# Graph layer on one core: the token term moves from TensorE matmuls to ScalarE pre-fills and GpSimd row additions

## The chip, the cores and the metric

The kernel runs on one core of a Trainium2 chip. The metric is the device time of one execution in microseconds (us); the time before is the median of three runs, 2477.9 us (2477.26 to 2478.84). Engines are named as in the profile: PE is TensorE's matmuls and PEld its weight loads, DVE is VectorE, ACT is ScalarE, POOL is GpSimd, SP is SyncE, which issues the DMAs.

## What is computed

There are 64 samples of 256 tokens with 768 features, and a 256x256 adjacency matrix for each. It is 0 or 1 here, and the same matrix serves as `heads` and as `rels`. Cut to what matters:

```python
h = relu(layernorm(x))
ctx = (adj  @ (h @ Wadj.T + badj)) / deg_c  + (radj @ (h @ Wrev.T + brev)) / rdeg_c
ctx = ctx + h @ Wself.T + bself
rel = agg @ Wr.T + br * deg + ragg @ Wrr.T + brr * rdeg     # agg = sum_j adj_ij * E[rels_ij]
out = x + ctx + rel
```

`deg` and `rdeg` are row sums of the adjacency and of its transpose, `deg_c` and `rdeg_c` the same with 0 replaced by 1. Since every edge has relation 1, `agg @ Wr.T` is the degree times one fixed row of 768 numbers (a row of `E` through `Wr`), and likewise for the reverse term. So beside the large products there is a **token term**: a row `bself`, a row `badj` where `deg > 0`, a row `brev` where `rdeg > 0`, and two rows multiplied by `deg` and by `rdeg`.

## The kernel before, in words

**Tiling and stages.** A sample has two blocks of 128 tokens, c = 0 and 1. For each there are three output blocks of 128x768, `c{c}{m}`: m = 0 is h Wadj, m = 1 the result with h Wself (it starts from x), m = 2 is h Wrev. The product of the 256x768 h with the three weight matrices is split by a bilinear scheme into 15 smaller products, each of three passes over words of split precision (4 matmuls a pass, 12 a product). The first sweep (`SWEEPS[0]`, 8 products) goes over all regular samples 1 to 62, its five partial blocks are kept in DRAM, then the prepared weight words are exchanged and the second sweep (`SWEEPS[1]`, 7 products) goes over all samples again and ends with the aggregation. Samples 0 and 63 are done whole, by plain matmuls (`whole`), sample 63 in the exchange between the sweeps.

**A product** (`product`): `split` makes the left words (ACT left0, DVE left1 and left2; in the second sweep the two DVE steps have two SBUF inputs, L613 and L617), PE runs the first passes into a PSUM bank, ACT rescales the bank in place (L666), PE adds the second passes (L628), and DVE or ACT reads the bank into the blocks (L676, L685, L687). Some left inputs are sums of two pieces that POOL makes first (`combine`, L590).

**The aggregation** (`high_low`, `aggregate`): a block is split in two words, the high one by ACT (L928) and the low one by POOL (L932). For each of two directions k and two token blocks ic, 8 matmuls (L944) of the adjacency with the words fill a bank, and DVE adds bank times 1/degree to the result block `c{ic}1` (L955). That is 32 matmuls a sample beside 84 of the seven products.

**The token term before.** `front2` puts 16 small columns (flags, ones, degrees) into `cols` (L910, L911), PE transposes them (L915), ACT copies the result as the token tile (L919). `add_rows` (L638) multiplies four 32-row tiles of it by `rows`, a tile made once in `rows_prepare`, into the banks of products 7 and 15 (v and u), after both of their passes; the second read of each of the two banks (`read(1)`) is held until then. Samples 0 and 63 get the term in banks of their own (L981).

**Order.** A planner (`Plan.schedule`) records all steps with a rank, a duration and the buffers they need, and emits one fixed order for each engine. The table `OFFSETS` shifts the rank of each kind of step. Steps marked `lock` (all of POOL's, and DVE's with two SBUF inputs) are never placed at the same time. `SLOTS` gives the number of buffers of a class: B are 128x768 blocks in SBUF, Q are PSUM banks in pairs. Semaphores keep the data dependencies at run time; each engine goes through its own order.

## Time and profile before

| what | value |
|---|---|
| median of three runs | 2477.9 us |
| the profiled execution: its own time | 2478.37 us |
| span of the profiled execution | 2476.5 us |
| outside the span | 1.87 us |
| PE busy, share | 2449.1 us, 99% |
| PEld busy, share | 2365.0 us, 95% |
| DVE, ACT, POOL busy, share | 85%, 72%, 52% |
| granted TensorE clock | 0.999 |

Busy times are unions of the instructions' intervals. PE's matmuls are pipelined, so a single one is shown longer than the distance to the next; what counts on PE is the distance between starts.

### The profile page before, as it was taken

The numbers are of one execution on the slowest core, as the hardware profiler recorded it, in microseconds if no ns is written. First come the engines' busy times: TensorE is split into PE (matmuls) and PEld (weight loads), VectorE is DVE, ScalarE is ACT, GpSimd is POOL, SyncE is SP. The second block draws the span as 40 slices with busy tenths as digits, with TensorE's granted clock in tenths as the row PEclk, the third lists the DMA queues.
The fourth block names the chain that finished last, engine by engine and source line by source line (L and its number), as shares of the span: only waits on it lengthen the run. The fifth ranks groups of instructions, "written<-read, shape, count | busy, mean of one in ns | idle before, by whom it ended". The sixth has DMA issues, their size and how long they took to land.

```text
span 2476.5 us, 43288 instructions
## 1 busy us (share of the span) xinstructions
PE 2449.1 (99%) x13858; PEld 2365.0 (95%) x13858; DVE 2096.0 (85%) x4003; ACT 1777.2 (72%) x3772; POOL 1283.1 (52%) x1138
## 2 busy tenths in 40 slices
PE   6999999999999999999999999999999999999998
PEld 4899999999999999996999999999999999999998
DVE  7887888788788878878988889888888888888987
ACT  4788888888888888886666666666666666666665
POOL 1555555555555555543555555555555555555554
PEclk9999999999999999999999999999999999999999
DMA  5677777777777777876666666666666666666664
GB/s 214 241 284 281 268 277 284 271 274 282 277 268 280 285 270 275 293 254 215 223 214 216 216 217 212 216 217 215 213 213 213 216 215 216 217 216 214 215 219 135
DMA packets 224776, 590.66 MB, mean 239 GB/s; under 512 B 25080, under 2 KB 25080, under 8 KB 224544
## 3 DMA queue, kind: packets, MB, share of 16 engines
q1 hardware_dynamic: 224544, 587.86, 69.5%
q8 instruction: 110, 1.80, 0.3%
q14 instruction: 122, 1.00, 0.1%
HBM read 364.28 MB, written 223.48 MB: 237 GB/s over the span
## 4 chain that ended last, share of the span: by engine, by line
PE 97%; DVE 1%; DMA 1%; ACT 1%; issue 0%; POOL 0%; SPq 0%; ACTq 0%; POOLq 0%
PE x L628 21%; PE y L628 21%; PE agg L944 14%; PE z L628 10%; PE w L628 10%; PE t L628 5%; PE v L628 5%; PE u L628 5%; PE whole L782 2%; PE v L638 1%; DMA raw<-in_Wself_dram 0%; PE right L502 0%; PE pt L915 0%; DMA row<-d 0%; DVE right L555 0%
## 5 line engine op out<-in xcount | busy, mean ns | idle before, releaser
L932 POOL TENSOR_TENSOR hl<-c,hl 128x768 fp32r<-128x768 f32 x256 | 474.7, 1855 | 646.3 <-ACT hl L928 470.6
L628 PE MATMUL x<-word,left 128*128 128x384 f32 x2976 | 589.3, 339 | 0.2 <-DVE c L687 0.2
L628 PE MATMUL y<-word,left 128*128 128x384 f32 x2976 | 569.3, 335 | 0.0
L628 PEld LDWEIGHTS x<-word,left 128*128 128x128 f32 x2976 | 515.2, 188 | 14.2 <-issue 11.0
L628 PEld LDWEIGHTS y<-word,left 128*128 128x128 f32 x2976 | 517.8, 188 | 5.2 <-ACT y L666 1.0
L944 PE MATMUL agg<-hl,a 128*128 128x384 f32 x2048 | 395.3, 334 | 0.0
L944 PEld LDWEIGHTS agg<-hl,a 128*128 128x128 f32 x2048 | 358.4, 188 | 0.6 <-issue 0.2
L745 POOL TENSOR_TENSOR h<-h,row 128x768 f32<-128x768 f32 x128 | 234.6, 1855 | 177.5 <-DMA row<-d 132.2
L628 PE MATMUL z<-word,left 128*128 128x384 f32 x1488 | 299.3, 335 | 0.7 <-DVE x L793 0.4
L628 PE MATMUL w<-word,left 128*128 128x384 f32 x1488 | 298.2, 334 | 0.2 <-ACT w L666 0.2
L666 ACT ACTIVATE x<-x 128x768 f32<-128x768 f32 x248 | 191.8, 794 | 137.1 <-PE x L628 136.4
L628 PEld LDWEIGHTS z<-word,left 128*128 128x128 f32 x1488 | 258.7, 188 | 4.5 <-DVE x L793 0.7
L628 PEld LDWEIGHTS w<-word,left 128*128 128x128 f32 x1488 | 261.3, 188 | 0.8 <-ACT w L666 0.5
L955 DVE SCALAR_TENSOR_TENSOR c<-agg,rd,c 128x768 f32<-128x768 f32 x252 | 255.2, 1013 | 7.1 <-PE agg L944 3.9
L928 ACT ACTIVATE hl<-c 128x768 fp32r<-128x768 f32 x256 | 215.2, 841 | 30.9 <-DVE c L685 25.0
L666 ACT ACTIVATE y<-y 128x768 f32<-128x768 f32 x248 | 197.1, 795 | 41.5 <-PE y L628 41.4
L722 POOL TENSOR_TENSOR cols<-cols,half 128x2 f32<-128x2 f32 x64 | 83.0, 1296 | 252.7 <-DVE cols L721 252.7
L617 DVE SCALAR_TENSOR_TENSOR left<-left,top 128x256 fp32r<-128x256 f32 x496 | 199.5, 413 | 6.4
L685 DVE TENSOR_TENSOR c<-c,v 128x768 f32<-128x768 f32 x124 | 117.5, 947 | 102.0 <-PE v L628 101.1
L617 DVE SCALAR_TENSOR_TENSOR left<-left 128x256 fp32r<-128x256 f32 x434 | 203.3, 490 | 0.1
L607 ACT ACTIVATE top<-left 128x256 f32<-128x256 f32 x496 | 181.0, 383 | 6.2 <-DVE left L617 2.0
L676 ACT ACTIVATE c<-y 128x768 f32<-128x768 f32 x124 | 101.1, 815 | 70.0 <-PE y L628 69.9
(136 smaller groups left out, 4308.3 us busy)
## 6 DMA issues: line engine op xcount, KB each, us to landing
c<-kept SPq DMA_DIRECT2D x316, 384.0 KB
kept<-c SPq DMA_DIRECT2D x252, 384.0 KB
x<-in_x_dram SPq DMA_DIRECT2D x128, 384.0 KB
h<-in_x_t_dram SPq DMA_DIRECT2D x128, 384.0 KB
out_dram<-c SPq DMA_DIRECT2D x126, 384.0 KB
kept_h<-h SPq DMA_DIRECT2D x124, 384.0 KB
h<-kept_h SPq DMA_DIRECT2D x124, 384.0 KB
adj<-in_adj_dram SPq DMA_DIRECT2D x64, 512.0 KB
```

The lines of the kernel that those rows point to most:

```text
L607: lambda: nc.scalar.activation(view(top), t(w)[:, 0].bitcast(F32), AF.Copy),
L617: lambda: nc.vector.scalar_tensor_tensor(t(w)[:, 2], t(w)[:, 1].bitcast(F32), -STEP, first(), op0=ALU.mult, op1=ALU.add), s == 1,
L628: nc.tensor.matmul(t(q)[:, half, : H // 2], t(w)[:, lw, f, :], t(r[rw])[:, f, ts(half, H // 2)], start=start and i == 0 and f == 0, stop=s ...
L666: lambda: nc.scalar.activation(view(), view(), AF.Copy, scale=scale),
L676: lambda o=o, sign=sign: nc.scalar.activation(t(o).rearrange("p (k n) -> p k n", k=2), view(), AF.Copy, scale=sign * (1.0 if value_last el ...
L685: emit = lambda to=to, op=op: nc.vector.tensor_tensor(to(), to(), view(), op=op)
L722: pool(0.7, r - 21.5, f"pow {b}", [col], [col], lambda: nc.gpsimd.tensor_tensor(var(), var(), v["half"], op=ALU.pow))
L745: lambda h=h, one=one: nc.gpsimd.tensor_tensor(t(h), t(h), one(0), op=ALU.subtract),
L928: lambda: nc.scalar.activation(t(pair)[:, 0], t(o), AF.Copy, scale=LOWER),
L932: lambda: nc.gpsimd.tensor_tensor(t(pair)[:, 1], t(o), t(pair)[:, 0].bitcast(F32), op=ALU.subtract),
L944: nc.tensor.matmul(t(q)[:, half, : H // 2], t(s["a"])[:, c, k, ts(ic, P)], t(pairs[c])[:, part, ts(half, H // 2)], start=(c == 0 and part ...
L955: lambda q=q, to=to, ic=ic: nc.vector.scalar_tensor_tensor(to(), t(q)[:, :, : H // 2], t(rd)[:, ic, k : k + 1], to(), op0=ALU.mult, op1=AL ...
```

## The change

PE's token rows, the transposes and the token tiles are gone. In their place: (1) in each of the four aggregation banks of a sample ACT first writes a prepared row (`forward` or `reverse`) times the squared degree, and the 8 matmuls accumulate on that; the later multiplication by 1/degree makes it row times degree. (2) ACT writes the row `brev` into the banks of products 7 and 15 before their first matmul. (3) POOL adds `badj` to the blocks c00 and c10 of regular samples in the first sweep, and `bself` minus `brev` to c01 and c11 in the second; for samples 0 and 63 it adds all bias rows. (4) DVE computes the squared degrees (`sqd`) in place of the two column steps. (5) Five rows of 128x768 are loaded by broadcast DMAs in place of one small 5-row load issued eight times, and hold five B buffers from then on; B has 19 slots in place of 18. (6) The second reads of products 7 and 15 are no longer held back. (7) `OFFSETS` is a new table (741 of the 749 kinds that stay have another value), and the planner may widen its look-ahead where it would find no order. The diff, cut:

```diff
-SLOTS = {"W": 24, "B": 18, "T": 5, "A": 3, "S": 6, "Q": 4, "U": 2}
+SLOTS = {"W": 24, "B": 19, "T": 5, "A": 3, "S": 6, "Q": 4, "U": 2}
...
+            if not events and pace < 1000.0:
+                pace *= 2.0
+                continue
+            pace = PACE
...
-    def add_rows(b, rank, token, qs, start):
...
+    def add_row(name, o, rank, what):
+        row = v["row"][name]
+        pool(
+            on_pool(H), rank, what, [row, o], [o],
+            lambda: nc.gpsimd.tensor_tensor(t(o), t(o), t(row), op=ALU.add),
+        )
+
+    def load_row(name, at, rank):
+        row = v["row"][name] = plan.buf("B", [P, H], F32, f"row_{name}")
+        dma(384, rank, "bias", [], [row], lambda: nc.sync.dma_start(t(row), v["bias"][at].partition_broadcast(P)))
+        return row
...
+        fresh = place == 0
+        if n in (7, 15):
+            row = v["row"]["brev"]
+            act(
+                in_place(H), rank - 1.0, f"init {n} {b}", [row], [q],
+                lambda: nc.scalar.activation(view(), t(row).rearrange("p (k n) -> p k n", k=2), AF.Copy),
+            )
+            fresh = False
...
+                if m == 0:
+                    add_row("badj", o, rank + 3.0, f"bias{c}{m} {b}")
                 return
...
+        brev, bself = load_row("brev", 1, rank - 8.0), load_row("bself", 2, rank - 8.0)
+        per = [load_row(name, 3 + k, rank - 8.0) for k, name in enumerate(("forward", "reverse"))]
...
-        dve(0.2, r - 2.0, f"tok {b}", degs, [(col, 0)], lambda: nc.vector.tensor_scalar(to(0), of(), 0.0, None, op0=ALU.is_gt))
-        dve(0.2, r - 2.0, f"tok {b}", degs, [(col, 1)], lambda: nc.vector.tensor_copy(to(3), of()))
+        dve(0.2, r - 2.0, f"sqd {b}", degs, [sqd], lambda: nc.vector.tensor_tensor(t(sqd), t(deg)[:, b], t(deg)[:, b], op=ALU.mult))
...
-        pt = plan.buf("Q", [P, 2, 512], F32, f"pt2_{b}")
-        pe(0.3, r - 1.0, f"turn2 {b}", [col], [pt], lambda: nc.tensor.transpose(t(pt)[:, 0, :P], t(col), v["ident"]))
-        s["token"] = v["tokens"][b % 2]
-        act(
-            0.3, r - 0.5, f"token {b}", [pt], [s["token"]],
-            lambda: nc.scalar.activation(t(s["token"]), t(pt)[:, 0, :P], AF.Copy),
-        )
...
-                                start=(c == 0 and part == 0), stop=(c == 1 and part == 1),
+                                start=False, stop=(c == 1 and part == 1), skip_group_check=True,
...
+            row, sqd = v["row"][("forward", "reverse")[k]], v["sqd"][b % 2]
+            act(
+                in_place(H), rank - 1.5 + 1.4 * ic, f"init{k}{ic} {b}", [row, sqd], [q],
+                lambda q=q, ic=ic, row=row: nc.scalar.activation(
+                    t(q)[:, :, : H // 2], t(row).rearrange("p (k n) -> p k n", k=2), AF.Copy, scale=t(sqd)[:, ic, k : k + 1]
+                ),
+            )
...
-                add_rows(b, r + 2.1 * i + 3.0, s["token"], [q for q, _ in held], False)
...
+            product(b, 1, spec, r + 2.1 * i, banks)
+        for c in range(C):
+            if b not in regular:
+                for m, name in ((0, "badj"), (2, "brev"), (1, "brev")):
+                    add_row(name, blocks[b, c, m], r + c - 2.0, f"bias{c}{m} {b}")
+            add_row("bself", blocks[b, c, 1], r + (6.0 * c + 3.0 if b in regular else c), f"self{c} {b}")
```

## Rows read from the trace of the kernel before

**Rows 1.** The page: the span, and the chain that ended last.
```profile
span 2476.5 us, 43288 instructions
PE 97%; DVE 1%; DMA 1%; ACT 1%; issue 0%; POOL 0%; SPq 0%; ACTq 0%; POOLq 0%
```

**Rows 2.** Busy time by stretch (first sweep, then second): PE, PEld, DVE, ACT, POOL.
```profile
400.00:800.00 400.00, 400.00 (x2305) 397.98 (x2304) 322.87 (x721) 337.17 (x673) 222.37 (x216) 1.00 0.77 277
1600.00:2000.00 400.00, 400.00 (x2326) 390.65 (x2325) 355.48 (x615) 258.91 (x595) 210.72 (x174) 1.00 0.67 215
```

**Rows 3.** Timeline of PE, second sweep: start us, us, engine, line, tiles.
```profile
1641.66 1.55 PE L944 MATMUL agg<-hl,a 128*128 128x384 f32 x8
1643.14 0.44 PE L638 MATMUL v<-rows,token 32*128 32x384 f32 x2
...
1643.52 1.67 PE L628 MATMUL x<-word,left 128*128 128x384 f32 x8
1645.03 1.55 PE L944 MATMUL agg<-hl,a 128*128 128x384 f32 x8
...
1651.27 2.24 PE L628 MATMUL x<-word,left 128*128 128x384 f32 x12
1653.35 1.55 PE L944 MATMUL agg<-hl,a 128*128 128x384 f32 x8
...
1659.59 0.86 PE L628 MATMUL v<-word,left 128*128 128x384 f32 x4
1660.28 0.27 PE L915 MATMUL pt<-ident,cols 128*128 128x128 f32 x1
1660.31 1.66 PE L628 MATMUL x<-word,left 128*128 128x384 f32 x8
1661.81 0.85 PE L628 MATMUL u<-word,left 128*128 128x384 f32 x4
...
1681.13 0.27 PE L915 MATMUL pt<-ident,cols 128*128 128x128 f32 x1
```

**Rows 4.** Groups by line and form: names, shapes xcount | busy us, mean ns | idle before.
```profile
L932 POOL TENSOR_TENSOR hl<-c,hl 128x768 fp32r<-128x768 f32 x256 | 474.7, 1855 | 646.3 <-ACT hl L928 470.6 <-DMA c<-in_x_dram 158.7 <-PE x L628 9.7
L928 ACT ACTIVATE hl<-c 128x768 fp32r<-128x768 f32 x256 | 215.2, 841 | 30.9 <-DVE c L685 25.0 <-DVE right L539 3.1 <-DVE c L687 2.3
L617 DVE SCALAR_TENSOR_TENSOR left<-left 128x256 fp32r<-128x256 f32 x434 | 203.3, 490 | 0.1
L607 ACT ACTIVATE top<-left 128x256 f32<-128x256 f32 x496 | 181.0, 383 | 6.2 <-DVE left L617 2.0 <-ACT left L600 0.3
L600 ACT ACTIVATE left<-h 128x256 fp32r<-128x256 f32 x248 | 101.4, 409 | 8.0 <-DMA out_dram<-c 5.3 <-DVE h L749 2.0 <-PE x L628 0.5
L919 ACT ACTIVATE token<-pt 128x128 fp32r<-128x128 f32 x64 | 17.8, 278 | 5.8 <-PE pt L915 5.8
L910 DVE TENSOR_SCALAR cols<-deg 128x16 f32<-128x16 f32 x64 | 13.6, 213 | 2.1 <-ACT a L898 2.1
L858 ACT ACTIVATE rows_rest<-brow,upper 128x768 f32<-128x768 f32 x1 | 0.9, 925 | 0.0
L855 ACT ACTIVATE rows_hi<-brow 128x768 fp32r<-128x768 f32 x1 | 0.8, 833 | 0.0
```

**Rows 5.** The line of left2: duration ns min/median/max of all.
```profile
L617 DVE SCALAR_TENSOR_TENSOR left<-left x434: 395/415/771, 1163.0 to 2455.2; 128x256 fp32r<-128x256 f32 x145
```

**Rows 6.** Timeline of all engines, second sweep: a POOL and a DVE instruction that meet.
```profile
1649.05 0.74 POOL L590 TENSOR_TENSOR b1+b<-h 128x256 f32<-128x256 f32 x1
1649.32 0.76 DVE L617 SCALAR_TENSOR_TENSOR left<-left 128x256 fp32r<-128x256 f32 x1
```

**Rows 7.** Waits of the weight loads' queue: who for whom, us in total, times, longest.
```profile
PEld v L638 <- DVE c L685: 15.0, 60, 0.3
```

**Rows 8.** The exchange between the sweeps: PE's timeline, and busy time.
```profile
1143.99 0.33 PE L915 MATMUL pt<-ident,cols 128*128 128x128 f32 x1 [1.13 <-DVE x L793]
1140.00:1200.00 60.00, 58.78 (x277) 46.94 (x276) 56.35 (x82) 35.99 (x80) 26.05 (x22) 1.00 0.61 209
```

More of the change, by code (lines that the diff above doesn't have):

```diff
@@ L632, in passes @@
                     )
-    def add_rows(b, rank, token, qs, start):
-        def run():
-            for g in range(4):
-                at = slice(32 * g, 32 * (g + 1))
-                nc.tensor.matmul(
-                    t(qs[g // 2])[:, g % 2, : H // 2], t(token)[at], t(v["rows"])[at, ts(g % 2, H // 2)],
-                    start=start, stop=True, skip_group_check=not start, tile_position=(32 * g, 0),
-                )
-        pe(0.55, rank, f"token rows {b}", [token, v["rows"], *qs], [*qs], run)
+    def add_row(name, o, rank, what):
[8 more added lines that the diff above has]
+        return row
     def product(b, s, spec, rank, banks):
@@ L690, in read @@
             dve(on_dve(H), rank + 2.5 + 0.5 * i, f"read {n} {b}", [q, o], [o], emit)
-        if s == 0 or n not in (7, 15):
-            for i in range(len(reads)):
-                read(i)
-            return
-        read(0)
-        return q, lambda: read(1)
+        for i in range(len(reads)):
+            read(i)
     def front1(b):
@@ L844, in picks @@
+        for k in range(2):
+            pr = plan.buf("Q", [P, 2, 512], F32, f"pr{k}")
+            def picks(k=k, pr=pr):
+                for n in range(2):
                     nc.tensor.matmul(
[L845 removed]
+                        t(pr)[:, n, : H // 2], t(pick)[:, k * P : (k + 1) * P], t(wr[k])[:, ts(n, H // 2)], start=True, stop=True
                     )
[L848 removed]
@@ L962, in step2 @@
         r = start2[b]
-        held = []
         for i, spec in enumerate(SWEEPS[1] if b in regular else ()):
-            more = product(b, 1, spec, r + 2.1 * i, banks)
-            if more:
-                held.append(more)
-            if len(held) == 2:
-                add_rows(b, r + 2.1 * i + 3.0, s["token"], [q for q, _ in held], False)
-                for _, read in held:
-                    read()
-                held = []
-        if b not in regular:
-            qs = [plan.buf("Q", [P, 2, 512], F32, f"rows{c}_{b}") for c in range(C)]
-            add_rows(b, r, s["token"], qs, True)
-            for c in range(C):
-                o = blocks[b, c, 1]
-                to = lambda o=o: t(o).rearrange("p (k n) -> p k n", k=2)
-                dve(
-                    on_dve(H), r + c + 1.0, f"rows{c} {b}", [qs[c], o], [o],
-                    lambda q=qs[c], to=to: nc.vector.tensor_tensor(to(), to(), t(q)[:, :, : H // 2], op=ALU.add),
-                )
+            product(b, 1, spec, r + 2.1 * i, banks)
[4 more added lines that the diff above has]
+            add_row("bself", blocks[b, c, 1], r + (6.0 * c + 3.0 if b in regular else c), f"self{c} {b}")
         at = lambda x: r + (x if b in regular else 0.5 * x - 2.0)
@@ L992, in step2 @@
             dma(384, at(24.0), f"out{c} {b}", [o], [], lambda o=o, c=c: nc.sync.dma_start(v["out"][b][:, c, :], t(o)))
-    if part is None:
+    v["row"] = {}
+    if part is not None:
+        v["row"] = {name: one for name in ("badj", "brev", "bself", "forward", "reverse")}
+    else:
+        load_row("badj", 0, start1[1])
         front1(0)
@@ L1096, in main_path @@
             "sq": own("sq", [P, B, C], F32),
-            "cols": [own(f"cols{i}", [P, P], F32) for i in range(2)],
-            "tokens": [own(f"token{i}", [P, P], F32R) for i in range(2)],
+            "cols": [own(f"cols{i}", [P, 32], F32) for i in range(2)],
+            "sqd": [own(f"sqd{i}", [P, C, 2], F32) for i in range(2)],
             "rd": [own(f"rd{i}", [P, C, 2], F32) for i in range(2)],
         }
+        small.tile([P, 24], F32, name="rest_of_256")
         for col in fixed["cols"]:
```

94 lines of the change are left out of this document (25 added, 69 removed), and 286 rows, old and new, of the table OFFSETS.

## The prediction, made before the changed kernel had run

> **What bounds the kernel now.** I read the chain that ended last first: PE holds 97% of it, no other engine more than 1% [rows 1]. Then the busy times by stretch, because the two sweeps differ: in a stretch of each, PE is busy 400.00 of 400 us. Beside it, in the first sweep DVE is at 81%, ACT 84%, POOL 56%; in the second DVE 89%, ACT 65%, POOL 53% [rows 2]. So nobody else is late by more than PE can cover, and the time is the sum of what PE issues. Last I read PE's timeline of one sample in the second sweep, to see what its issues cost. The reader should look at starts, not durations: twelve matmuls of a product begin at 1651.27 and the next group at 1653.35, so one takes 2.08/12 = 0.1733 us [rows 3]. From transpose to transpose a sample takes 1681.13 - 1660.28 = 20.85 us [rows 3]; its 116 large matmuls (84 of the products, 32 of the aggregation) make 20.11. The rest, 0.74 us, must be the token term.
>
> **Removed from PE.** Eight aggregation matmuls start at 1641.66 and should end their slot at 1643.05; the token rows start at 1643.14 and the next product at 1643.52, which is 0.47 us. The eight matmuls behind them then take 1.51 us to the next group instead of 8 x 0.1733 = 1.39, another 0.12 [rows 3]. The token rows thus cost 0.59 us, though each shows 0.44 and they run side by side. The transpose takes 0.03 us itself, and the eight behind it take 1.50 instead of 1.39: 0.14 in all [rows 3]. The sum, 0.73, closes the gap of 0.74. For 62 regular samples this is 45.3 us; samples 0 and 63 have the same steps, 1.5 more: 46.8 us. All of it lies on the path, since PE has no idle time here. Part of the 0.47 is the wait of the first token weight load for DVE's read, 15.0 us over 60 samples, 0.25 each [rows 7]; it goes with the instruction, because the second reads are no longer a condition for anything on PE. The picks of `rows_prepare` stay as many matmuls.
>
> The sum is made against the profiled execution: 2478.37 us, which is the span of 2476.5 plus 1.87 around it, 0.5 us above the median of 2477.9. The floor is 2478.4 - 46.8 = **2431.6 us**.
>
> **Added to ACT.** No row shows a 128x768 pre-fill from SBUF to PSUM. The nearest is `top`, 128x256 to PSUM, 383 ns; 512 more columns cost 841 - 409 = 432 ns by the two SBUF forms [rows 4], so some 815 ns. The four aggregation fills take their scale from a tile; the one pair of rows with and without such a scale differs by 925 - 833 = 92 ns [rows 4], so 907. A sample gets 2 x 815 + 4 x 907 = 5.26 us and loses the token copy of 0.28 [rows 4]. ACT's 258.91/400 x 20.85 = 13.50 us [rows 2] become 18.5 of 20.11, 92%. It doesn't become the bound, but it is fuller than any engine beside PE is now. More than the sum, the place matters: each fill puts an ACT step between a bank's last read and PE's next matmul in it, so behind an ACT queue that waits for PE's passes (L666) there stands a fill for which PE waits later. Where the fill comes late, PE stalls. The nearest row for a PE wait on a result that comes just in time is again 0.25 us, once a sample [rows 7]. Bounds: no wait, since PE's order can put another product between, and one wait for each of the six fills, 1.5 us a sample or 93 us. I take half of one wait, 0.12 us a sample, **7.5 us**: nearest to the present order, in which PE waits at no other place more than a few times.
>
> **Added to POOL, and what it does to DVE.** Two additions a sample of the size of L932, 1855 ns each [rows 4], in each sweep. In the second POOL goes from 210.72/400 x 20.85 = 10.98 us to 14.69 of 20.11 (73%), in the first from 9.25 to 12.96 of 96 x 0.1733 = 16.64 (78%) [rows 2]. POOL has the room. The price is paid elsewhere: a DVE step with two SBUF inputs that started at 1649.32, while POOL worked from 1649.05 to 1649.79, ended only at 1650.08, 0.29 us after POOL, and took 0.76 us [rows 6] against a median of 415 ns [rows 5]. Over 434 such steps the mean is 490 [rows 4], so 75 ns too much, 0.53 us a sample. Growing with POOL's work this becomes 0.71, 0.18 more. Queued behind the blocked step on DVE are the bank reads, and for those PE waits. DVE's own work is 355.48/400 x 20.85 = 18.53 us [rows 2], less one column step of 0.21 (L910, [rows 4]; its partner is exchanged for `sqd`): 18.3, so 18.5 of 20.11, 92%. Bounds: nothing, if the order keeps the two apart as the planner's lock wants, and 2 x 1.855 = 3.71 us, if each addition blocks a DVE step for its whole length. I take the 0.18, which DVE's free time covers: 0 us on the path. In the first sweep DVE has only the two norm steps of this kind and 3.2 us free a sample; there I charge 0, with one wait of 0.25 us a sample (15.5 us) as the other end. That sweep gains nothing, so anything that comes there is a pure loss.
>
> The Trainium skill has a rule that speaks against this part: SBUF — State Buffer, "Who interferes with whom", says that GpSimd and a DVE instruction with two SBUF inputs hold the shared port pair exclusively, each for its whole instruction, and the second blocks. The trace agrees in kind: 0.76 us against 0.415 in the pair of rows above.
>
> **Buffers, loads and the ends.** B has 19 slots; `badj` takes one in the first sweep, so 18 stay as before. In the second, five rows take the place of one, so 14 stay where 17 were. No row shows free slots; bounds are nothing and the same 0.25 us a sample. I charge nothing: an earlier read of v and u frees banks and blocks in return. At the exchange, four broadcast loads of 384 KB are 1.57 MB. The DMA queues move 209 GB/s there at a share of 0.61 [rows 8], so at most some 343 GB/s, which makes it 4.6 us of queue time, in a stretch where 39% of 60 us is free; the eight small bias loads go. Samples 0 and 63 get 16 POOL additions, 29.7 us, where POOL is idle 34 of 60 us [rows 8]. They stand before the words of their aggregations, and behind them POOL's own low words and pair sums are queued. The bounds are -1 us (PE's only wait there, 1.13 us, stands before a transpose that goes [rows 8]) and two additions for each sample in a row, 7.4. I take **2 us**. Opening and tail keep their steps; nothing is charged.
>
> Forecast: 2431.6 + 7.5 + 2 = **2441 us**; its own range is 2431 to 2450.
>
> **Rivals.**
>
> *The port is the bound.* If POOL and the 14 two-input DVE steps of a sample can never overlap at all, a sample needs 14.69 + 14 x 0.415 = 20.50 us of this one resource, more than PE's 20.11, and loses 0.39 x 62 = 24 us: 2456 (2450 to 2466). This is what the skill's rule just named would make of it. Against it: a DVE step behind POOL ended 0.29 us after it [rows 6]; with this per step the sum is 18.8, below PE's. For it: even so the pair is taken for 93% of the time, and the pieces must fit.
>
> *The fills come late.* Three waits of 0.25 us a sample for the six fills give back 0.75 us x 62 = 46 us: 2478 (2466 to 2490), no change. For it: ACT at 92%, and two engines above 90% at once, which no stretch shows now. Against: at 84% ACT in the first sweep, PE is busy 400.00 of 400 [rows 2].
>
> *DVE is blocked and becomes the bound, slower.* With the full 3.71 us DVE needs 18.3 + 3.7 = 22.0 us a sample, 1.15 above the 20.85 of now: +71 us, with the gain of samples 0 and 63 some 2548. It decides from 20.85 - 18.3 = 2.55 us of blocking a sample, that is where each addition holds DVE up for over 1.3 of its 1.855 us. Midway, at 3.1, it is (21.4 - 20.85) x 62 = 34 us above now: 2512 (2485 to 2548). For it: DVE goes through a fixed order, and its next bank read waits behind the blocked step. Against: now a step loses 75 ns on the average though POOL works more than half of the time.
>
> *The first sweep loses.* One wait of 0.25 us a sample for a POOL addition that stands in front of a pair sum: 2441 + 15.5 = 2457.
>
> **How the numbers follow.** Forecast 0.40; port 0.15; late fills 0.18; DVE blocked 0.22; first sweep 0.05. A measurement of this kernel can tell about 0.2%, 5 us, from no change, so "same" is 2473 to 2483. From the late fills I put 0.04 below that, 0.09 inside, 0.05 above. Faster: 0.40 + 0.15 + 0.05 + 0.04 = 0.64; same 0.09; slower 0.22 + 0.05 = 0.27. The range is 2430 to 2505: below it lies 0.03, above it some two thirds of the case of the blocked DVE, 0.14.
>
> **What would show it.** Right: in the second sweep a sample of 20.1 to 20.3 us between the same matmuls, no L638 or L915, PE still busy all the time there and in the first sweep, ACT near 18 and POOL near 14.7 us a sample, fills of 0.8 and 0.9 us. The port shows in a longer mean of L617 and L613 with PE idle before passes whose left words come late; late fills show in weight loads of agg, v and u that wait for ACT; a blocked DVE in bank reads that start long after PE and in DVE above 95%. A first sweep over 16.7 us a sample would make my zero there wrong. The forecast is wrong if PE's share in the second sweep falls below 98%.

## The result, and the profile after

The changed kernel takes 2600.29 us (median; 2599.71 to 2602.18) where the kernel before took 2478.21 beside it: a ratio of **1.049** [1.048, 1.051], 122 us slower, and 159 us above the forecast. The page of after, with its span, busy shares and the chain that ended last:

```profile
span 2599.1 us, 43889 instructions
PE 2479.5 (95%) x13538; PEld 2341.8 (90%) x13538; DVE 2337.0 (90%) x3915; ACT 2071.8 (80%) x4086; POOL 1766.8 (68%) x1401
PE 73%; DVE 17%; issue 3%; ACT 3%; DMA 2%; POOL 1%; DVEq 0%; ACTq 0%; SPq 0%; POOLq 0%
```

Of the chain, 17% is now DVE, where it was 1% [rows 1]. The same two stretches as in [rows 2], with the same columns (PE, PEld, DVE, ACT, POOL, granted clock, DMA share, GB/s):

```profile
400.00:800.00 400.00, 400.00 (x2306) 398.83 (x2305) 350.98 (x724) 340.75 (x673) 295.53 (x265) 1.00 0.81 277
1600.00:2000.00 400.00, 375.84 (x2052) 351.62 (x2051) 380.62 (x548) 318.83 (x640) 267.92 (x193) 1.00 0.60 200
```

The first sweep still has PE busy for all of its 400 us, with 73 us more POOL work in it. The second has lost it: PE 400.00 to 375.84, and DVE is at 380.62 of 400, 95%. The clock is 1.00, so the loss is waiting. The mean distance between the first aggregations of successive samples (samples 5 to 55, worked out from the starts) is 22.64 us, where it was 20.83: 1.81 more for each of 62 samples is 112 of the 122 us.

PE's timeline of one sample in the second sweep, with the idle time before an instruction and its releaser in brackets:

```profile
1802.20 1.69 PE L918 MATMUL agg<-hl,a 128*128 128x384 f32 x8 [0.81 <-ACT agg L926]
1804.07 1.66 PE L629 MATMUL t<-word,left 128*128 128x384 f32 x8 [0.17 <-DVE c L936]
...
1811.15 0.97 PE L629 MATMUL x<-word,left 128*128 128x384 f32 x4 [0.56 <-DVE c L697]
...
1818.77 0.96 PE L629 MATMUL v<-word,left 128*128 128x384 f32 x4 [0.25 <-ACT v L676]
...
1825.42 1.67 PE L918 MATMUL agg<-hl,a 128*128 128x384 f32 x8 [0.81 <-ACT agg L926]
```

The token rows and the transpose of [rows 3] are gone, and waits stand in several places instead: for a fill (L926), for DVE's reads of a bank (L936, L697), for a rescale (L676). PE no longer waits for one thing; what these have in common has to be looked for on the engines behind them. DVE, the same few microseconds, beside POOL and the fill:

```profile
1806.30 3.65 POOL L906 TENSOR_TENSOR hl<-c,hl 128x768 fp32r<-128x768 f32 x2
1806.33 1.01 DVE L936 SCALAR_TENSOR_TENSOR c<-agg,rd,c 128x768 f32<-128x768 f32 x1
1807.26 0.91 DVE L892 TENSOR_TENSOR sqd<-deg 128x4 f32<-128x4 f32 x1
1808.09 2.14 DVE L618 SCALAR_TENSOR_TENSOR left<-left 128x256 fp32r<-128x256 f32 x1
1810.15 0.94 DVE L697 TENSOR_TENSOR c<-c,x 128x768 f32<-128x768 f32 x1
```

POOL makes two low words, from 1806.30 to 1809.95. L936, one of whose inputs is a PSUM bank, runs through them. `sqd`, a 128x4 step with both inputs in SBUF, needs 0.91 us; the left2 behind it 2.14, and it ends at 1810.23, 0.28 us after POOL. The read that stands behind it, L697, then comes late, and that read is what PE waits for at 1811.15 (the x bank). So the timeline has the mechanism of [rows 6], but behind POOL's long instructions and on steps of no size. The groups by line and form say how much of this there is (xcount | busy us, mean ns of one):

```profile
L618 DVE SCALAR_TENSOR_TENSOR left<-left 128x256 fp32r<-128x256 f32 x434 | 267.1, 639 | 0.0
L892 DVE TENSOR_TENSOR sqd<-deg 128x4 f32<-128x4 f32 x64 | 70.9, 1108 | 2.2 <-ACT a L882 2.2
L614 DVE TENSOR_TENSOR left<-h,left 128x256 fp32r<-128x256 f32 x124 | 69.1, 558 | 0.0
L893 DVE TENSOR_SCALAR rd<-deg 128x4 f32<-128x4 f32 x64 | 54.7, 855 | 0.0
L614 DVE TENSOR_TENSOR left<-a0+a,left 128x256 fp32r<-128x256 f32 x62 | 45.8, 738 | 0.0
L894 DVE RECIPROCAL rd<-rd 128x4 f32<-128x4 f32 x64 | 10.6, 166 | 0.1
```

Against the 415 ns of an undisturbed left step [rows 5], seven L618 lose 1.57 us a sample, two `h,left` 0.29, one `a0+a` 0.32. `sqd` could be done in 130 ns (its shortest) and loses 0.98, `rd` in 156 and loses 0.70; the reciprocal of the same size, 166, loses nothing. Together 3.9 us a sample, where the prediction had found 0.53. DVE's own 18.3 holds that 0.53 already, so DVE comes to 18.3 - 0.53 + 3.9 = 21.7 us a sample; the stretch has 380.62/400 x 22.64 = 21.5. That is 95% of the 22.64 that a sample takes, so DVE's sum alone doesn't give the time either.

In what follows, "blocked" is the sum, over the DVE instructions that start between 1600 and 2000 us, of the time above the short (5th percentile) duration of their kind, where that is over 0.05 us: 11.6 us before, 51.9 after (a low count for after, since nearly all its `rd` are long). By the sample this is 0.60 and 2.94 us. Of the 51.9, 36.2 end with a low word of POOL, which before had too; nearly none with the new additions.

### The profile page after: what moved, and what is told of

It reads as the page before. It is cut to its first block, busy times and chain, and to the rows that moved or that the text cites. A ratio compares the mean times of both kernels' runs of the same rounds, so it can differ in the third digit from the quotient of the medians.

```text
span 2599.1 us, 43889 instructions
## 1 busy us (share of the span) xinstructions
PE 2479.5 (95%) x13538; PEld 2341.8 (90%) x13538; DVE 2337.0 (90%) x3915; ACT 2071.8 (80%) x4086; POOL 1766.8 (68%) x1401
## 4 chain that ended last, share of the span: by engine, by line
PE 73%; DVE 17%; issue 3%; ACT 3%; DMA 2%; POOL 1%; DVEq 0%; ACTq 0%; SPq 0%; POOLq 0%
PE y L629 19%; PE x L629 14%; PE w L629 9%; PE z L629 9%; PE agg L918 7%; PE v L629 6%; PE t L629 5%; DVE c L936 4%; DVE left L614 3%; PE whole L790 3%; DVE c L697 3%; DVE c L699 2%; ACT v L676 2%; DVE left L618 2%; DVE rd L893 2%
## 5 line engine op out<-in xcount | busy, mean ns | idle before, releaser
L906 POOL TENSOR_TENSOR hl<-c,hl 128x768 fp32r<-128x768 f32 x256 | 498.1, 1965 | 153.4 <-issue 122.1
L629 PE MATMUL x<-word,left 128*128 128x384 f32 x2976 | 577.2, 337 | 7.8 <-ACT x L676 3.6
L629 PE MATMUL y<-word,left 128*128 128x384 f32 x2976 | 579.6, 335 | 1.8 <-DVE c L699 1.1
L918 PE MATMUL agg<-hl,a 128*128 128x384 f32 x2048 | 405.9, 340 | 42.5 <-ACT agg L926 42.2
L639 POOL TENSOR_TENSOR c<-c,row_badj 128x768 f32<-128x768 f32 x128 | 238.4, 1863 | 185.5 <-ACT c L686 143.8
L936 DVE SCALAR_TENSOR_TENSOR c<-agg,rd,c 128x768 f32<-128x768 f32 x252 | 254.3, 1010 | 19.8 <-POOL c L639 16.6
L618 DVE SCALAR_TENSOR_TENSOR left<-left 128x256 fp32r<-128x256 f32 x434 | 267.1, 639 | 0.0
L639 POOL TENSOR_TENSOR c<-c,row_bself 128x768 f32<-128x768 f32 x126 | 230.4, 1850 | 25.7 <-DVE c L697 25.5
L676 ACT ACTIVATE y<-y 128x768 f32<-128x768 f32 x248 | 196.4, 792 | 57.4 <-PE y L629 57.4
L902 ACT ACTIVATE hl<-c 128x768 fp32r<-128x768 f32 x256 | 207.0, 832 | 11.2 <-POOL c L639 8.2
L676 ACT ACTIVATE x<-x 128x768 f32<-128x768 f32 x248 | 197.1, 795 | 22.4 <-PE x L629 21.3
L608 ACT ACTIVATE top<-left 128x256 f32<-128x256 f32 x496 | 189.6, 383 | 22.0 <-DVE left L618 19.8
L618 DVE SCALAR_TENSOR_TENSOR left<-left,top 128x256 fp32r<-128x256 f32 x496 | 200.7, 415 | 6.6
L591 POOL TENSOR_TENSOR a1+a<-h 128x256 f32<-128x256 f32 x62 | 48.3, 780 | 205.7 <-DMA h<-kept_h 149.9
```

The costliest lines, as they stand in the source:

```text
L608: lambda: nc.scalar.activation(view(top), t(w)[:, 0].bitcast(F32), AF.Copy),
L618: lambda: nc.vector.scalar_tensor_tensor(t(w)[:, 2], t(w)[:, 1].bitcast(F32), -STEP, first(), op0=ALU.mult, op1=ALU.add), s == 1,
L629: nc.tensor.matmul(t(q)[:, half, : H // 2], t(w)[:, lw, f, :], t(r[rw])[:, f, ts(half, H // 2)], start=start and i == 0 and f == 0, stop=s ...
L639: lambda: nc.gpsimd.tensor_tensor(t(o), t(o), t(row), op=ALU.add),
L676: lambda: nc.scalar.activation(view(), view(), AF.Copy, scale=scale),
L902: lambda: nc.scalar.activation(t(pair)[:, 0], t(o), AF.Copy, scale=LOWER),
```

## The experiments

Each was compared with the kernel before on the same chip. "Sample" is the mean distance of first aggregations as above.

### Does PE get its time back?

Before's order, with the token work left out:

```diff
-        pe(0.55, rank, f"token rows {b}", [token, v["rows"], *qs], [*qs], run)
+        pe(0.55, rank, f"token rows {b}", [token, v["rows"], *qs], [*qs], lambda: None)
...
-        pe(0.3, r - 1.0, f"turn2 {b}", [col], [pt], lambda: nc.tensor.transpose(t(pt)[:, 0, :P], t(col), v["ident"]))
+        pe(0.3, r - 1.0, f"turn2 {b}", [col], [pt], lambda: None)
...
```

> The kernel before, in its own order, with the token rows, the transposes, the token copies and the column steps left out, so the output lacks the token term. All theories: this measures the gain alone. If it is 0.73 us a sample, the time is 2478 - 47 = 2431 us, and a sample of the second sweep takes 20.1 us instead of 20.83. If another engine or a load is right behind PE, less than half of it: above 2455.

Measured: 2451.81 us, ratio 0.989 [0.986, 0.992]; sample 20.44. The stretch and the waits of the weight loads in it (total us, times, longest):

```profile
1600.00:2000.00 400.00, 398.72 (x2273) 393.20 (x2272) 350.90 (x587) 258.81 (x587) 213.95 (x177) 1.00 0.69 219
PEld agg L944 <- PE x L628: 6.8, 19, 0.4
```

The gain is there, but 0.39 us a sample, not 0.73. In 400 us there are 19.6 samples, and each has one weight load that waits, 6.8/19.6 = 0.35 us: just what is missing. So something else in the loop takes 20.44 us too; what, can't be read from a wait that is put down to PE itself. That is the best this order gives, before any cost of what replaces the token rows.

### Does reading by POOL cost PE time, in an order that was in step?

Before's order again; two unused 128x4 DVE steps a sample, each behind a low word:

```diff
...
+                m == 2 and b in regular
+                and nc.vector.tensor_tensor(t(v["probe"]), t(v["deg"])[:, b], t(v["deg"])[:, b], op=ALU.mult),
...
```

> The kernel before in its own order, with one more DVE step of 128x4 with two SBUF inputs issued behind two of the four low words of each regular sample (its result is not used). It measures the price of such a step by itself. Theory A: each takes 1 us or more where it meets POOL instead of 0.17, what stands behind it is late too, and the time rises by 20 us or more. Theory C: the time stays within 6 us of 2478.

Measured: 2546.00, ratio 1.027 [1.024, 1.030]; sample 21.99, 1.16 more.

```profile
1600.00:2000.00 400.00, 384.67 (x2204) 369.98 (x2203) 356.50 (x621) 247.13 (x567) 198.80 (x164) 1.00 0.64 204
L935 DVE TENSOR_TENSOR probe<-deg 128x4 f32<-128x4 f32 x124 | 102.0, 822 | 0.0
```

Nothing waits for the result, and POOL and PE have the work of before. The step's mean is 822 ns, where `sqd` took 130 at its shortest: some 1.4 us blocked a sample, of which 1.16 arrive on PE. DVE had 11% of its time free and covered little of it.

The other half, more reading on POOL: the order without token work, and two unused additions of 128x768 a regular sample:

```diff
...
+                c == 1 and b in regular
+                and nc.gpsimd.tensor_tensor(
+                    t(v["rows"]), t(v["rows"]).bitcast(F32), t(v["rows"]).bitcast(F32), op=ALU.add
+                ),
...
```

> As b_no_token (2452 us), with two more GpSimd additions of 128x768 in each regular sample of the second sweep, issued behind two of the four low words, on a tile that nobody reads, so no result hangs on them. Theory A: DVE steps that the order of before kept clear of POOL now meet it, the excess rises from 0.3 to 1.5 us a sample or more, and the time to 2490 us or more. Theory C: POOL has 9 us a sample free, so below 2465 us.

Measured: 2680.76, ratio 1.082 [1.079, 1.085]; sample 24.11 (most take 23.95, a few some 25.3).

```profile
1600.00:2000.00 400.00, 352.30 (x1939) 337.68 (x1938) 355.92 (x499) 225.49 (x500) 236.54 (x183) 0.99 0.58 186
PEld x L628 <- DVE c L961: 37.6, 16, 2.4
```

3.67 us more than the 20.44 without them, where the two additions take 3.7. They are written behind the low words, at a place that no planner chose, so this is an upper end for additions; but POOL is busy for 237 of 400 us, and still a sample is late by nearly all that was put on it. The blocked time goes from 6.2 to 43.8 us, and PE's weight loads wait for DVE's read of the aggregation bank. The timeline has the chain:

```profile
1807.72 2.11 DVE L617 SCALAR_TENSOR_TENSOR left<-left 128x256 fp32r<-128x256 f32 x2
1807.88 1.66 POOL L935 TENSOR_TENSOR rows<-rows 128x768 fp32r<-128x768 f32 x1
1809.51 2.00 POOL L933 TENSOR_TENSOR hl<-c,hl 128x768 fp32r<-128x768 f32 x1
1809.76 2.04 DVE L613 TENSOR_TENSOR left<-a0+a2+b,left 128x256 fp32r<-128x256 f32 x1
1811.72 1.00 DVE L961 SCALAR_TENSOR_TENSOR c<-agg,rd,c 128x768 f32<-128x768 f32 x1
1812.78 1.36 PEld L628 LDWEIGHTS x<-word,left 128*128 128x128 f32 x8 [2.34 <-DVE c L961]
```

A left2 step ends 0.29 us behind the unused addition (L935), a left1 step 0.29 us behind the low word after it, and only then comes the read for which PE has waited 2.34 us. Those waits, 37.6 us for 16 samples, make 2.3 of the 3.67; what the additions cost by standing in POOL's own queue isn't told apart in the rest. A run with two of the four low words made twice was to show the same:

> As b_no_token, and two of the four low words of a sample are computed twice (the second writes the same values again), so that POOL works 3.7 us more a sample in the second sweep, the size of the two row additions, in the order of before. Theory A (two-input DVE steps blocked behind POOL): the excess of such DVE steps rises from 0.58 us a sample to 2 or more, and PE waits: over 2460 us. Theory B (fills come late) and theory C (the order and the fewer B buffers): POOL has the room, so within 8 us of b_no_token.

It took 2874.47, ratio 1.160 [1.156, 1.163], sample 27.31, but the doubled words also lengthen the path from a low word to its aggregation, and the granted clock fell to 0.87 in the stretch, where PE was idle for 56 of 400 us. Its sign agrees; its size can't be laid to blocking.

### Which new part is it, in the order of after?

Four runs take parts out of the changed kernel and keep its order. "Theory A" of their expectations is blocking, B late fills, C the order itself with its fewer buffers. The `bself` additions of regular samples left out:

```diff
-            lambda: nc.gpsimd.tensor_tensor(t(o), t(o), t(row), op=ALU.add),
+            (lambda: None) if what.startswith("self") and int(what.split()[1]) in regular
+            else lambda: nc.gpsimd.tensor_tensor(t(o), t(o), t(row), op=ALU.add),
```

> The changed kernel in its own order, with the two bself additions of each regular sample left out (output without that row). Theory A: POOL falls by 3.7 us a sample, low words come earlier and clear of DVE's steps, so the time falls by 40 us or more, from 2600 to below 2560. Theories B and C: less than 15 us.

The six fills left out (each bank is started by its first matmul):

```diff
-                lambda: nc.scalar.activation(view(), t(row).rearrange("p (k n) -> p k n", k=2), AF.Copy),
...
+                lambda: None,
...
-                                start=False, stop=(c == 1 and part == 1), skip_group_check=True,
+                                start=(c == 0 and part == 0), stop=(c == 1 and part == 1),
...
```

> The changed kernel in its own order, with the six fills of each sample left out (the first matmul overwrites; output without those rows). Theory B: PE's waits for ACT go, and the time falls by 80 us or more, below 2520. Theory A: DVE stays blocked, so less than 30 us. Theory C: less than 15 us.

The two small steps off DVE, `sqd` to ACT and the maximum of `rd` to POOL; and this with the `bself` additions left out as well:

```diff
-        dve(0.2, r - 2.0, f"sqd {b}", degs, [sqd], lambda: nc.vector.tensor_tensor(t(sqd), t(deg)[:, b], t(deg)[:, b], op=ALU.mult))
-        dve(0.2, r - 2.0, f"rd {b}", degs, [rd], lambda: nc.vector.tensor_scalar(t(rd), t(deg)[:, b], 1.0, None, op0=ALU.max))
+        dve(0.2, r - 2.0, f"sqd {b}", degs, [sqd], lambda: nc.scalar.activation(t(sqd), t(deg)[:, b], AF.Square))
+        dve(0.2, r - 2.0, f"rd {b}", degs, [rd], lambda: nc.gpsimd.tensor_scalar(t(rd), t(deg)[:, b], 1.0, None, op0=ALU.max))
```

> The changed kernel in its own order, with the two small steps that DVE does behind POOL, the squares (0.98 us in the median, with two SBUF inputs) and the maximum of the degrees (0.88 us), put into ScalarE's and GpSimd's queues at the same places. Theory A (two-input and small DVE steps blocked behind POOL start the delay): the excess of DVE steps falls from 3.6 to below 2 us a sample, a sample from 22.64 to 21.9 or less, the time to 2555 us or less. Theory C (the order itself, made with fewer buffers, is late): less than 20 us.

> As a_small_off_dve, and the two bself additions of each regular sample are left out. Theory A: both sources of blocking are gone, the time is below 2530 us. Theory C: within 30 us of the 2590 us that the kernel without the additions took.

| run | us | ratio | sample | blocked, us of 400 |
|---|---|---|---|---|
| after | 2600.29 | 1.049 | 22.64 | 51.9 |
| no `bself` additions | 2590.12 | 1.045 [1.041, 1.050] | 22.44 | 50.5 |
| no fills | 2587.42 | 1.044 [1.041, 1.047] | 22.35 | 53.2 |
| small steps off DVE | 2591.63 | 1.046 [1.043, 1.049] | 22.54 | 70.9 |
| both small steps and additions | 2588.09 | 1.044 [1.041, 1.047] | 22.46 | 74.1 |

Each is worth 9 to 13 us of 122 (for two of them the interval still touches that of after, 1.048 to 1.051), and two together no more than one. Theory A had put the runs without additions, without small steps and without both below 2560, 2555 and 2530 us, and theory B the run without fills below 2520: all missed, and all four came out as theory C said. None of the parts is the cause by itself. The small steps show one reason. With them gone, their 1.7 us a sample don't come free (though POOL now spends 0.37 on the maximum); the left2 steps take over:

```profile
L618 DVE SCALAR_TENSOR_TENSOR left<-left 128x256 fp32r<-128x256 f32 x434 | 348.9, 828 | 0.0
```

828 ns against 639. Whatever step with two SBUF inputs DVE has next when a low word begins is the one that is blocked. And without the fills, PE's weight loads wait 23.4 us in the stretch for DVE's reads of the aggregation banks (last line), where in after they had waited 13.0 for those and 15.9 for the fills: mostly the fills were late because DVE's reads before them were.

```profile
PEld agg L918 <- ACT agg L926: 15.9, 17, 1.1
PEld t L629 <- DVE c L936: 13.0, 18, 1.5
```
```profile
PEld t L629 <- DVE c L933: 23.4, 18, 1.9
```

### The low words, and the buffers

The order of after, the low words written as zeros without reading anything (so the aggregation lacks its low words):

```diff
-lambda: nc.gpsimd.tensor_tensor(t(pair)[:, 1], t(o), t(pair)[:, 0].bitcast(F32), op=ALU.subtract)
+lambda: nc.gpsimd.memset(t(pair)[:, 1].bitcast(F32), 0.0)
```

> The changed kernel in its own order, with the four low words of each sample written as zeros by a GpSimd memset that reads nothing, in place of the subtraction (the output loses the low words). The rows put 36 of 52 us of blocked DVE time in 400 us behind these low words. Theory A (blocking alone keeps the second sweep late): DVE's excess falls below 1.5 us a sample and a sample from 22.64 to 20.6 us or less, 2475 us in all. Theory C (the order itself is late, whatever DVE waits for): a sample stays above 21.6 us, over 2535 us in all, though DVE is hardly blocked any more.

Measured: 2565.60, ratio 1.035 [1.032, 1.038]; sample 22.22, blocked 31.5.

```profile
1600.00:2000.00 400.00, 382.19 (x2084) 357.13 (x2084) 351.65 (x558) 321.04 (x648) 189.85 (x198) 1.00 0.59 201
L618 DVE SCALAR_TENSOR_TENSOR left<-left 128x256 fp32r<-128x256 f32 x434 | 191.0, 464 | 0.0
L893 DVE TENSOR_SCALAR rd<-deg 128x4 f32<-128x4 f32 x64 | 13.9, 217 | 0.0
L892 DVE TENSOR_TENSOR sqd<-deg 128x4 f32<-128x4 f32 x64 | 12.1, 189 | 1.3 <-ACT a L882 1.3
SPq L859 <- PE v L629: 150.7, 18, 9.0
```

With a low word that only writes, `sqd` goes from 1108 to 189 ns, left2 from 639 to 464, and DVE from 380.62 to 351.65 us. It isn't only that the steps now fall elsewhere. Here one with two SBUF inputs starts inside two low words and stays short:

```profile
1806.74 1.42 POOL L906 MEMSET hl<- 128x768 f32 x2 [0.78 <-PE agg L918]
1807.51 0.42 DVE L614 TENSOR_TENSOR left<-h,left 128x256 fp32r<-128x256 f32 x1
```

So do 30 `sqd` steps, at most 158 ns each, and 136 left2 steps, at most 421 (those that lie over a low word and over no other instruction of POOL). `rd` goes from 855 to 217, but no `rd` lies over a write alone here, so for it only the meetings are gone. The run is worth 35 us, and not all of that need be blocking, for a written word also takes 0.71 us of POOL in place of 1.96, which shortens the way to the aggregation. It came out on theory C's side (over 21.6 us a sample). DVE is at 88% and PE still idle, so something else is late now. The last line of the first view is SP's queue: the load of `h` (L859) waits 8.4 us a sample for PE to be done with a buffer; in after the same line stands at 123.5 us and 17 times. Behind it, POOL's pair sums wait for that load (114 us in the stretch). So the buffers that the rows hold (14 left of 17) seem to cost. Two runs give three of them back, by letting rows share a tile (so the token term is wrong there) and handing out all B buffers as they come free, two things that the runs don't tell apart; with this the second sweep begins some 26 to 28 us later, which their times contain:

```diff
+        alias = {"row_brev": "row_badj", "row_bself": "row_badj", "row_reverse": "row_forward"}
...
+                        b.tile = named[alias[b.name]].tile
```

> The changed kernel with every engine's order kept, but with three more B buffers for the blocks in the second sweep: the rows badj, brev and bself (all zeros here) share one tile and the reverse row shares the forward one, which makes the output's reverse term wrong. Buffers then come free earlier; 17 are left, as before the change. In the trace of the changed kernel the load of h waits 8.1 us a sample, in SyncE's queue, for PE's second passes of v, that is for a buffer. Theory C1 (a loop through the buffers: passes of v, load of h, pair sum, left words, passes): these waits go and a sample takes 21.9 us or less instead of 22.64, the time is below 2555 us. Theory C2 (the engines' orders hook into each other whatever the buffers): less than 15 us. Theory A (blocking): less than 20 us, as the blocking stays.

> As a_slots, and the low words are written by a GpSimd memset that reads nothing, as in a_low_memset (2566 us). If blocking behind POOL and the loop through the buffers are together all of the loss, a sample comes to 20.1 to 20.5 us and the time to 2440 to 2460 us. If the orders hook into each other apart from that (C2), a sample stays above 21.2 us, over 2510 us.

Measured: with buffers alone 2684.61, ratio 1.083 [1.080, 1.086], sample 23.65, *slower* than after; with buffers and low words that don't read, 2526.42, ratio 1.019 [1.016, 1.022], sample 21.03. The stretch of each, in this order:

```profile
1600.00:2000.00 400.00, 359.31 (x1965) 336.85 (x1964) 382.34 (x525) 307.80 (x608) 251.73 (x187) 1.00 0.54 190
```
```profile
1600.00:2000.00 400.00, 395.31 (x2208) 379.24 (x2208) 353.67 (x591) 340.66 (x687) 200.05 (x210) 1.00 0.60 213
```

So neither cause alone explains after. With the low words reading, the buffers bring nothing: neither the gain expected from a loop through the buffers came nor "no change"; the steps meet worse here (left2 at 847 ns, 54.5 us blocked). With both changes a sample falls from 22.64 to 21.03, 1.61 of the 1.81 that were lost, and PE is nearly full again. Of that 1.19 came with the buffers, but the blocked time fell with them as well, from 31.5 to 14.1 us, so this isn't the price of buffers alone. It lies between the two expectations: above the 20.1 to 20.5 us of a loss that is all blocking and buffers, below the 21.2 of orders that hook into each other apart from that.

### The same fills and buffers in an order without meetings

The last three runs ask whether the fills and the held buffers cost PE time wherever they stand. They have another table of ranks, chosen so that GpSimd's reads and the two-input steps of DVE fall apart, `sqd` on ACT, and no `bself` additions for regular samples; everything else of the changed kernel stays, the `badj` additions of the first sweep too.

```diff
-    "a0+a1+b0+b1": -58.86, "a0+a1+b0+b1$1": -18.64, "a0+a1+b0+b1@1": -19.73, "a0+a2": 1.68, "a0+a2$1": 1.54,
+    "a0+a1+b0+b1": -48.42, "a0+a1+b0+b1$1": -18.15, "a0+a1+b0+b1@1": -19.73, "a0+a2": 7.46, "a0+a2$1": 4.35,
...
-        dve(0.2, r - 2.0, f"sqd {b}", degs, [sqd], lambda: nc.vector.tensor_tensor(t(sqd), t(deg)[:, b], t(deg)[:, b], op=ALU.mult))
+        act(0.2, r - 2.0, f"sqd {b}", degs, [sqd], lambda: nc.scalar.activation(t(sqd), t(deg)[:, b], AF.Square))
...
-            add_row("bself", blocks[b, c, 1], r + (6.0 * c + 3.0 if b in regular else c), f"self{c} {b}")
+            if b not in regular:
+                add_row("bself", blocks[b, c, 1], r + c, f"self{c} {b}")
```

> The changed kernel with another order (a table of ranks searched so that no two-input DVE step stands beside an instruction of GpSimd that reads), the squares of degrees on ScalarE, and the additions of bself to regular samples left out, so that the second sweep has no addition of a row; fills, row buffers and the badj additions of the first sweep stay. Theory (meetings of GpSimd's reads with two-input steps are the cause): the blocked time falls below 15 us in 400, and a sample of the second sweep takes 20.2 to 20.6 us as without token work; the exchange is some 20 us longer in this order, so 2450 to 2485 us. Rival (the six fills, or the buffers that the rows hold, cost PE time wherever they stand): a sample of 21.5 us or more, 2520 us or more, although little is blocked.

Measured: sample 20.55 us, 1.0 us blocked in 400; 2498.92 us, ratio 1.009 [1.007, 1.010].

```profile
1600.00:2000.00 400.00, 400.00 (x2262) 390.63 (x2261) 359.01 (x587) 354.11 (x720) 218.52 (x175) 1.00 0.66 217
PEld agg L918 <- ACT agg L926: 4.6, 20, 0.2
PEld x L629 <- issue: 4.2, 19, 0.2
```

PE is full again with all six fills, ACT at 354 of 400 and the rows in 5 B buffers. This is 0.11 us a sample above the 20.44 without any token work, in another order. Against the 20.11 of PE's matmuls it is 0.44 more, and two waits make that up: one for a fill, 4.6 us or 0.24 a sample, and one that the profile puts down to nobody, 0.22. Each sample is 0.28 shorter than before. The kernel is slower all the same (2490.88 to 2502.38 us in four runs; the trace is that of the first): the first sweep ends 14 us later (1136.0 against 1121.9), and what is left of the sweep's gain, 62 x 0.28 = 17 us, goes in its first and last samples: from its first product to its last it takes 1289.1 us, as before (1288.4). Whether 20.55 can be had together with the ends of before, no run shows.

The two `bself` additions back, placed by the planner with the same table:

> The kernel g_order with the two bself additions of a sample back in the second sweep, placed by the planner with the same table. It computes all that the changed kernel computes. Theory (meetings): that table leaves no gap for 3.7 us of reading on GpSimd, so two-input steps are blocked again: a sample of 22.5 to 25 us, 2600 to 2750 us, blocked over 40 us in 400. Rival (additions cost little, as leaving them out of the changed kernel gave only 10 us): within 15 us of g_order.

Measured: 2676.90 us, ratio 1.080 [1.078, 1.082]; sample 23.49, blocked 27.0.

```profile
1600.00:2000.00 400.00, 369.78 (x2005) 351.90 (x2006) 331.13 (x518) 311.36 (x634) 254.98 (x189) 0.98 0.58 193
PEld x L629 <- DVE left L618: 21.5, 9, 2.4
```

2.94 us a sample for 3.7 us of additions, somewhat less than in the order without token work (3.67). In the order of after leaving them out gave 0.20, since there the steps met anyway. The size wasn't as expected: 27.0 us blocked are 1.6 us a sample (27.0/400 x 23.49), and DVE is busy for only 331 of 400 us. So here a part of the loss is not blocking; PE waits for left words, and whether these stand behind pair sums that queue behind the additions on POOL I didn't separate.

And `sqd` back on DVE, without the additions:

> The kernel g_order with the squares of degrees on DVE again, one 128x4 two-input step a sample. Theory (a small step is blocked as long as a large one, and passes it on to PE): 0.3 to 0.6 us a sample more than g_order, 20 to 40 us, though the step takes 0.13 us by itself. Rival (only DVE's sum counts): 0.13 us a sample in DVE's free time, within 5 us of g_order.

Measured: 2511.35 us, ratio 1.013 [1.011, 1.015], 12 us more than the median of g_order and 9 more than its slowest run; sample 20.78. The step, 0.13 us by itself and 0.20 here, comes with 0.23 us a sample of PE's time:

```profile
1600.00:2000.00 400.00, 395.90 (x2233) 385.07 (x2231) 355.23 (x599) 343.75 (x696) 214.17 (x173) 1.00 0.66 215
L892 DVE TENSOR_TENSOR sqd<-deg 128x4 f32<-128x4 f32 x64 | 13.0, 203 | 4.7 <-ACT a L882 4.7
```

It is less than expected, and `sqd` itself is hardly blocked. The planner put the others elsewhere, and now they are: 15.0 us blocked against 1.0, 10.0 of it behind low words. That is more than the rival's "nothing", and it is an effect of the order.

## Why the prediction was wrong, by its steps

**What bounds the kernel** held: PE without idle time, in both sweeps. It was read as "nobody else is late by more than PE can cover". PE has nothing to cover with, and that the others have free time doesn't say that a delay on them stays there. Two unused steps of 0.13 us, lengthened to 0.82, went through to PE with 1.16 us a sample.

**Removed from PE**: 0.73 us a sample by the starts; 0.39 measured with nothing in its place, because a weight load then waits 0.35 us.

**Added to ACT**: the prices were right. The fills take these (predicted 907 and 815 ns):

```profile
L926 ACT ACTIVATE agg<-row_forward,sqd 128x768 f32<-128x768 f32 x128 | 115.8, 905 | 81.7 <-DVE c L936 42.4 <-DVE c L697 39.3
L668 ACT ACTIVATE u<-row_brev 128x768 f32<-128x768 f32 x62 | 50.9, 821 | 0.0
```

ACT has 318.83/400 x 22.64 = 18.0 us a sample, as forecast. The waits for fills were put at 0.12 us a sample. In after weight loads wait 15.9 us for them in the stretch, 0.90 a sample, but leaving the fills out gave 0.29 back: mostly they passed on a delay of DVE's. In an order almost without meetings one such wait of 0.24 is left. So the term was half of that, too small by some 7 us, and that isn't what failed.

**Added to POOL** is the step that failed. The additions cost 1850 and 1863 ns as predicted, and POOL's room was there. The failure is the sentence "growing with POOL's work this becomes 0.71, 0.18 more", together with "which DVE's free time covers". The blocked time didn't grow with POOL's work by a third, it grew from 0.53 to 3.9 us a sample by the groups (0.60 to 2.94 by the stretch). The 3.4 more are near the bound of 3.71 that was meant for the worst case, but the bound looked at the two additions, and hardly any of the blocking ends with those. Three things were missed. Most of the blocking comes from low words that were there before: the low rate of before was a property of an order in which the two engines' steps fell apart, not a rate per microsecond of POOL's work. The 128x4 steps count as much as large ones, for they wait as long: `sqd`, which was charged as an exchange for a column step of 0.21 us, takes 1.11. And the free time of DVE doesn't cover a delay, since the reads that PE waits for stand behind it.

The Trainium skill (SBUF — State Buffer, "Who interferes with whom") states the rule: GpSimd's reads and a DVE instruction with two SBUF inputs exclude each other for a whole instruction, and an instruction that only writes doesn't count. The runs agree: the same 128x4 step takes 1108 ns in the mean beside low words that read, and at most 158 where it lies over one that only writes. The prediction had cited the rule and set its price from one average.

**The order.** The meeting of steps counts more than the sum of any engine. Two things speak for it: blocked time moves to other steps when some are taken away (small steps off DVE), and with another table the same fills, buffers and low words meet for 1.0 us in 400 and PE is full. That table has `sqd` on ACT and no `bself` additions, and it changes everything else in the order too, so it shows that the rest of the change can run in step, and not that meetings are all that was wrong with the order of after. The two additions found no place: put once into each of two orders that were in step they cost 3.67 and 2.94 us a sample, and the whole change took 2592 us at best (small steps off DVE). How much of the 1.81 in the order of after is due to each is not to be told, since there the parts stand in for one another. So what is shown is that blocked steps reach PE, in orders where nothing else was changed; that they and the buffers make most of the loss of after rests on the one run that took out both, and that made the low words shorter as well. Why that order meets, with a lock in its plan, isn't shown either: `sqd` and `rd` carry no lock in it (`front2`), but with both off DVE hardly anything was gained.

**Buffers** were charged nothing, with 0.25 us a sample as the other end. Their price depends on the order: in that of after up to 1.19 us with most of the blocking gone, and nothing to be had while it is there; in the order almost without meetings PE has no wait that is put down to them.

**The exchange** was charged 2 us. The second sweep's first product starts 2.3 us earlier than before (1172.66 against 1174.95), and behind its last the kernel takes 15.3 us in place of 13.2; the sweep itself has the rest, 1411.1 against 1288.4.

**The first sweep** was charged nothing, and that was right: PE 400.00 of 400, though there too a small DVE step is blocked, `eps` (ns, shortest, median, longest):

```profile
L729 DVE TENSOR_SCALAR cols<-cols x64: 160/1334/1698, 6.5 to 1085.6; 128x2 f32<-128x2 f32 x64
```

Its median was 163 before. By its rank it stands 13 us ahead of the norm step that needs it (`front1`), and so 1.2 us cost nothing.

**The rivals.** "DVE is blocked and becomes the bound" is what came: DVE at 95%, bank reads late. It decided from 2.55 us of blocking more than DVE's 18.3; some 3.4 came, by the groups, though not from the additions. Its top, 2548, was too low because it let DVE work without a pause: a sample takes 22.64 us with DVE busy for 21.5, for DVE too waits for others in the loop. "The port is the bound" had the right resource, but taken as a sum it gave 2456; the loss is in the meetings. The signs named in the last part (longer means of the left lines, DVE above 95%, PE below 98%) were the ones that came.

## What to carry to other kernels

When an engine is full and its neighbours run in step with it, cost a new GpSimd instruction by the DVE steps with two SBUF inputs that it can meet, the smallest ones included, each for what is left of the GpSimd instruction, and take DVE's free time as cover only where the step has time to spare ahead of its reader. Small one-input steps of `tensor_scalar` count too, as `rd` and `eps` did here. A low average of such meetings in the trace before belongs to that order and can't be scaled. And where several causes hold the same queue up, taking one away shows little: put each alone into an order that runs in step.

## What the runs showed of the hardware

The size of a DVE step doesn't matter for how long it is blocked, and one step can be passed over more than once. In the exchange of after (timeline of DVE and POOL):

```profile
1140.08 1.83 POOL L906 TENSOR_TENSOR hl<-c,hl 128x768 fp32r<-128x768 f32 x1
1140.88 4.60 DVE L892 TENSOR_TENSOR sqd<-deg 128x4 f32<-128x4 f32 x1 [2.16 <-ACT a L882]
1141.85 1.85 POOL L639 TENSOR_TENSOR c<-c,row_badj 128x768 f32<-128x768 f32 x1
1143.62 1.83 POOL L639 TENSOR_TENSOR c<-c,row_bself 128x768 f32<-128x768 f32 x1
```

A step of 0.13 us ends at 1145.48, 0.03 behind the third of three instructions of POOL. Over all that were blocked in after, the small steps end 0.02 us (`sqd`, median of 60) and 0.03 us (`rd`, 61) behind an instruction of POOL, left2 0.28 us (67), as in [rows 6]. An input from PSUM spares a step (L936 runs through two low words in 1.01 us). One input alone doesn't: the maximum of `rd`, from one 128x4 tile, goes from 156 to 855 ns, while the reciprocal of the same size stays at 166, also where it starts inside an instruction of POOL (12 times, at most 179). And a POOL instruction that only writes leaves the steps with two SBUF inputs short: `sqd` at most 158 ns, left2 at most 421 where they lie over a memset. For `rd` no run shows that.
